# One group of accumulating matmuls moved behind the next step's first transposes in a selective-scan network

## The chip, the cores and the metric

The kernel runs as one program on one core of a Trainium2 chip. The metric is the device time of one execution in microseconds (us), lower is better. A core has five engines that run their own instruction streams and meet at semaphores: TensorE (PE; its weight loads are a row of their own, PEld), VectorE (DVE), ScalarE (ACT), GpSimd (POOL) and SyncE (SP), which issues the DMAs here.

## The reference

Four layers work on an image batch of shape (4, 64, 64, 96). Layers 0 and 1 are two-dimensional selective-scan blocks: a projection in, a 3x3 depthwise convolution, four scans over the 4,096 (or 64 x 33) positions in four directions, a normalization, a gate and a projection out. Layer 1 does this on the image's Fourier transform. Layers 2 and 3 are linear attention and a quantized feed-forward network on the tokens. The scan is what the change touches:

```python
def step(hst, inputs):
    ul, dl, bl, cl = inputs
    dA = jnp.exp(dl[..., None] * A)
    hst = hst * dA + (dl * ul)[..., None] * bl[:, :, None, :]
    y = jnp.einsum('bkdn,bkn->bkd', hst, cl)
    return (hst, y)
```

Every channel d has 16 states n. For each state the recurrence h = h·a + b runs along the positions, with a = exp(delta·A) and b = delta·u·B; the output y is the sum over the 16 states of h·C.

## The kernel before, in words

**Tiling.** Each direction is cut into segments of 512 positions (layer 1: 512, 512, 384, 384 and 320). There are 144 segments. Channels lie on the 128 partitions, in three chunks c. A segment's 16 states are worked in four quarters q of four states j = 0 to 3. A step is one (segment, q, c): four states of one chunk over one segment. There are 144 x 4 x 3 = 1,728 steps, run by one loop (L843), in six phases: two for layer 0 (two images each) and four for layer 1 (one image each).

**What a step needs.** For j = 0 and 1, b is made on ScalarE with positions on the partitions (`make_bx`, L636) and turned round by TensorE: `transposed(st, j)` (L674, matmuls at L678) writes it into a PSUM tile, four matmuls of 128x128 for 512 positions, three for the shorter segments. For j = 2 and 3, b is a product on GpSimd (`front_b`, L695, work at L700). ScalarE makes a with exponentials (L682). VectorE runs the four recurrences one after another (`scan`, L704, work at L710).

**What becomes of h.** The result of j = 0 stays in its PSUM tile. VectorE multiplies it with C (`multiply_kept`, L725, work at L728) into the tile hk, which has two buffers, and ScalarE keeps its last column as the state for the next segment (`keep_state`, L730, work at L735). In every second step of layer 0, and every fourth of layer 1, j = 3 is treated in the same way (`kept`, L519); these are 624 steps. The other states are multiplied on GpSimd (`multiply`, L737, work at L747). TensorE sums all products in a PSUM accumulator `acc`, one per chunk: `add_kept` (L771) for hk, `add_rest` (L766) for GpSimd's products; both call `accumulate` (L749), whose matmuls are at L757 and turn the data back to positions on partitions by passing it against the identity. After the last quarter, `close_chunk` (L783) copies `acc` out (L788) and stores it.

**PSUM tiles.** The b of j = 0 and 1 and the a of j = 2 and 3 share three PSUM tiles in turn (`room`, L671), four uses a step. So the next step's first transposes write into the tile that this step's second scan (j = 1) has read, and its second transposes into the one that the third scan (j = 2) has read. The tile h of GpSimd's products has three buffers: `front_b` for step i+1 writes the buffer of step i-2, which `add_rest` must have read.

**What sets the order.** The order on TensorE, VectorE, ScalarE and GpSimd is written out by hand: the loop from L843 calls each piece where its instruction is to stand, and every engine works through its queue in that order. Only SyncE's order is chosen by the framework. In step i, TensorE's queue holds, from L871: `add_rest` of step i-2; `add_kept` of j = 3 of step i-1, where it has one; `add_kept` of j = 0 of step i (L882); what the first side slot brings (L897); the transposes j = 0 of step i+1 (L899); what the second side slot brings (L902); the transposes j = 1 of step i+1 (L904); what the third side slot brings (L911).

**Side slots.** `slot` (L820) issues work of everything that isn't a scan: preparing the next segment (`prepare`, L553, among it transposes at L612 which ScalarE copies at L615) and a phase's side tasks (projection, convolution, gates, the layers 2 and 3 of another image), at a rate per phase (RATES, L27). A side task yields after each piece; what a piece's matmuls made is read by another engine in a later slot.

Of the kernel before, what the change touches and what calls it, by code (L numbers as in the profile page):

```python
# [523 lines left out]
def scans(tc, ctx, phases, ident):  # L524
# [105 lines left out]
    def fetch_b(z, q):  # L630
        z.b[q] = broadcast(z, 4 * q + 2, 2, 0)

    def fetch_c(z, q):
        z.c[q] = broadcast(z, 4 * q, 4, 1)

    def make_bx(z, q):  # L636

        NI, PI, M, R = z.cfg.NI, z.cfg.PI, z.cfg.M, z.cfg.R
        for j in range(2):
            t = sp.tile([P, NBK, C, P], F32, name=f"bx_{z.nm}_{q}_{j}", tag="bx", bufs=4)  # L640
            z.bx[q, j] = t
            for b, (_, n) in enumerate(z.blocks):
                for i in range(NI):
                    m = i * M + R + 4 * q + j
                    ch = slice(i * PI, (i + 1) * PI)
                    nc.scalar.activation(  # L646
                        t[:n, b, :, ch], z.dut[:n, b, :, ch], AF.Copy, scale=z.bt[:n, b, m : m + 1]
                    )
                    yield
# [15 lines left out]
    def drain(gen):  # L665
        for _ in gen:
            pass
# [3 lines left out]
    def room(st, j):  # L671
        return ps.tile([P, 512], F32, name=f"ab_{st.nm}_{j}", tag=f"ab{next(turn) % 3}")

    def transposed(st, j):  # L674

        pb = st.px[j] = room(st, j)
        for b, (t, n) in enumerate(st.z.blocks):
            nc.tensor.transpose(pb[:, t : t + n], st.z.bx[st.q, j][:n, b, st.c], ident[:n, :n])  # L678
# [7 lines left out]
    def front_x(st):  # L686
        st.ax = sp.tile([P, 2, SM], F32, name=f"ax_{st.nm}", tag="ax", bufs=2)
        for j in range(2):
            exp(st.ax[:, j, : st.z.S], st, 4 * st.q + j)

    def front_y(st, j):
        st.ay[j] = room(st, j)
        exp(st.ay[j][:, : st.z.S], st, 4 * st.q + j)

    def front_b(st):  # L695

        S = st.z.S
        st.h = sp.tile([P, 3, SM], F32, name=f"h_{st.nm}", tag="h", bufs=3)
        for j in range(2):
            nc.gpsimd.tensor_tensor(  # L700
                st.h[:, 1 + j, :S], st.z.du[:, st.c, :S], st.z.b[st.q][:, j, :S], ALU.mult
            )
# [27 lines left out]
    def keep_state(st, j):  # L730
        z = st.z
        n = 4 * st.q + j
        if not z.last:
            e = last(z)
            nc.scalar.copy(z.state[st.c][:, n : n + 1], kept_at(st, j)[:, e : e + 1])  # L735
# [13 lines left out]
    def accumulate(st, hc, first=False, last=False):  # L749
        z = st.z  # L750
        if first:
            z.acc[st.c] = ps.tile([P, 512], F32, name=f"acc_{z.nm}_{st.c}", tag=f"acc{st.c}").rearrange(
                "p (b d) -> p b d", b=NBK
            )
        blocks = list(enumerate(z.blocks))
        for b, (t, m) in blocks[:: -1 if last else 1]:
            nc.tensor.matmul(  # L757
                z.acc[st.c][:m, b, :],
                hc[:, t : t + m],
                ident,  # L760
                start=(first and b == 0),
                stop=(last and b == 0),
                is_transpose=True,
            )

    def add_rest(st):  # L766
        m = 4 - len(st.kept)
        for j in range(m):
            accumulate(st, st.h[:, j], last=(st.q == NQ - 1 and j == m - 1))

    def add_kept(st, j):  # L771
        accumulate(st, st.hk[j], first=(st.q == 0 and j == 0))

    def open_segment(z, before):

        if z.first:
            z.state = [
                sp.tile([P, NST], F32, name=f"state_{z.nm}_{c}", tag=f"state{c}", bufs=2) for c in range(C)
            ]
        else:  # L780
            z.state = before.state
# [17 lines left out]
    with tc.manual_schedule(engines=IN_ORDER):  # L799
        drain(prepare(segs[0]))  # L800
        drain(make_bx(segs[0], 0))
        fetch_b(segs[0], 0)
        fetch_c(segs[0], 0)
        st = steps[0]
        for j in range(2):
            transposed(st, j)
        front_x(st)
        front_b(st)
        before = older = None
        more, pgen, pwants, at, due = Pieces(segs[0], 1, 4), none, None, 0, 0.0  # L810

        def prepare_more(kind):

            nonlocal pwants
            if pwants not in (None, kind):
                return False
            pwants = next(pgen, LATE)
            return True

        def slot(kind, hold=False):  # L820


            nonlocal due
            if hold:
                E.flush()
                return
            prepare_more(kind)
            due = min(due + st.z.ph.rate / 3, 3.0)
            for _ in range(min(int(due), 1 + (due >= 2.0))):
                due -= E.step(kind)  # L830

        def burst():

            if BURST in (pwants, E.wants):
                E.flush()
            if pwants is BURST:
                return prepare_more(BURST)
            if E.wants is BURST:
                E.step(BURST)
                return True  # L840
            return False

        for i, st in enumerate(steps):  # L843
            z, q, c, S = st.z, st.q, st.c, st.z.S
            nxt = steps[i + 1] if i + 1 < len(steps) else None
            if q == 0 and c == 0:
                after = z.after
                fresh = at == 0 or z.ph is not segs[at - 1].ph
                if fresh:
                    z.ph.io["y"] = [z.blk.dram_tile(f"y{j}", (2, z.cfg.L, C * P), z.ph.g) for j in range(2)]  # L850
                open_segment(z, segs[at - 1] if at else None)
                if after:
                    E.require(after.ph.needs[after.k % 2])
                pgen, pwants = prepare(after) if after else none, None
                at += 1
            if fresh and q == 0 and c == C - 1:
                for fn, arg in z.ph.side:
                    E.add((fn, arg), fn(E, arg))
            if c == 0:
                if q + 1 < NQ:  # L860
                    fetch_b(z, q + 1)
                elif after:
                    drain(pgen)
                    more = Pieces(after, 0, 4)
                    fetch_b(after, 0)
            if c == 1:
                if q + 1 < NQ:
                    fetch_c(z, q + 1)
                elif after:
                    fetch_c(after, 0)  # L870
            if older:  # L871
                add_rest(older)
            if before and 3 in before.kept:
                keep_state(before, 3)
                add_kept(before, 3)
            scan(st, 0)
            front_y(st, 2)
            if nxt:
                front_x(nxt)
            multiply_kept(st, 0)  # L880
            keep_state(st, 0)
            add_kept(st, 0)  # L882
            front_y(st, 3)
            long = burst()
            if before:
                multiply(before)
            if nxt:
                front_b(nxt)
            scan(st, 1)
            if nxt:  # L890
                if c == C - 1:
                    drain(more.gen)
                    if q + 2 < NQ:
                        more = Pieces(z, q + 2, 6)
                    elif q + 1 == NQ:
                        more = Pieces(nxt.z, 1, 6)
            slot(None)  # L897
            if nxt:
                transposed(nxt, 0)  # L899
            more.take(skip=long)  # L900
            scan(st, 2)
            slot(None, hold=long)  # L902
            if nxt:
                transposed(nxt, 1)  # L904
            if older and older.q == NQ - 1:
                close_chunk(older)
            scan(st, 3)
            if 3 in st.kept:
                multiply_kept(st, 3)
            more.take(skip=long and c == C - 1)  # L910
            slot(LATE)  # L911
            older, before = before, st
        multiply(before)
        if 3 in before.kept:
            add_kept(before, 3)
        for st in (older, before):
            add_rest(st)
            close_chunk(st)
        E.finish()
# [703 lines left out]
```

## Time and profile before

| What | us |
|---|---|
| median of 3 runs | 11260.47 |
| lowest and highest | 11260.01 and 11280.23 |
| the profiled execution | 11260.07 |
| its span, from first to last instruction | 11258.3 |
| TensorE: matmuls, weight loads busy | 9023.4, 6618.2 |
| VectorE, ScalarE, GpSimd busy | 9756.0, 9354.2, 9614.9 |
| matmuls of L757 from hk (seen as hk_l, k_l, _l) | 4760 + 3628 + 300 |
| matmuls of L757 from h | 16656 |
| matmuls of L678 | 6886 + 5312 + 474 |
| median of one matmul of L757, of L678 | 0.273, 0.273 |

Layer 0's phases begin at about 216 and 2,687 us, layer 1's at 5,130, 6,582, 7,997 and 9,431 us. Ahead of the first step there is only layer 0's first projection and convolution, behind the last (about 10,880 us) the end of the last image.

A row of the profile gives engine, line and operation, the output and inputs by their tile names without numbers, and a duration. The tile hk appears as hk_l, k_l or _l, and the tiles of `room` as ab_l, b_l or _l, since names are cut at the left: they are one kind of tile each. A wait is put down to the instruction whose semaphore came last. Durations of neighbouring matmuls overlap: four in a row at L678 or L757 take 0.60 us together in the median, not four times 0.273.

### The profile page before, as it was taken

How to read it: one execution, taken by the hardware profiler on the slowest of the kernel's cores; microseconds unless marked ns; L12 is line 12 of the kernel's file. 1: busy time of each engine (PE TensorE's matmuls, PEld its weight loads, DVE VectorE, ACT ScalarE, POOL GpSimd, SP SyncE). 2: the span in 40 equal slices, each digit the busy share in tenths (PEclk: the TensorE clock that was granted, in tenths of full speed). 3: DMA queues.
4: the chain of work that ended last, by engine and by line, in shares of the span. 5: the costliest groups of instructions: out<-in, count | busy, mean ns of one | idle time of the engine just before them, and what ended most of it. 6: DMA issues, size and time to landing. Idle time of an engine off the chain costs nothing. (4 is left out here: it accounts for less than half of the span.)

```text
span 11258.3 us, 163664 instructions
## 1 busy us (share of the span) xinstructions
PE 9023.4 (80%) x54944; PEld 6618.2 (59%) x54944; DVE 9756.0 (87%) x10419; ACT 9354.2 (83%) x19456; POOL 9614.9 (85%) x7464
## 2 busy tenths in 40 slices
PE   6678788777888888888888888887788777887775
PEld 2555555555667666656665665655556555655554
DVE  6889999889999998999888787988988889789864
ACT  3779999998898998998778788879888888778853
POOL 2999999888998998999789798988989889889860
PEclk8889999888998998999889899998899888899887
DMA  4655554555665556555554444542244322542242
GB/s 146 146 131 128 133 131 120 153 158 143 163 162 134 137 138 144 133 144 161 154 141 131 128 135 137 172 118 92 96 138 143 102 92 98 157 125 96 82 131 40
DMA packets 1205139, 1466.87 MB, mean 130 GB/s; under 512 B 480839, under 2 KB 1017295, under 8 KB 1145799
## 3 DMA queue, kind: packets, MB, share of 16 engines
q1 hardware_dynamic: 1204295, 1456.40, 47.7%
q8 instruction: 434, 7.11, 0.3%
q14 instruction: 410, 3.36, 0.1%
HBM read 1219.66 MB, written 236.50 MB: 129 GB/s over the span
## 5 line engine op out<-in xcount | busy, mean ns | idle before, releaser
L747 POOL TENSOR_TENSOR h_l<-h_l,bc_l 128x1536 f32<-128x1536 f32 (+2 forms) x1728 | 4784.4, 2769 | 192.1 <-DVE h_l L710 73.1
L700 POOL TENSOR_TENSOR h_l<-du_l,bc_l 128x512 f32<-128x512 f32 (+2 forms) x3456 | 3970.4, 1172 | 620.1 <-PE acc_l L757 581.1
L646 ACT ACTIVATE bx_l<-dut_l,bt_l 128x192 f32<-128x192 f32 (+2 forms) x6272 | 2754.6, 499 | 0.3
L757 PE MATMUL acc_l<-ident,h_l 128*128 128x128 f32 (+1 forms) x16656 | 2430.6, 299 | 243.5 <-POOL h_l L747 242.1
L757 PEld LDWEIGHTS acc_l<-ident,h_l 128*128 128x128 f32 (+1 forms) x16656 | 2130.9, 154 | 836.8 <-POOL h_l L747 384.9
L682 ACT ACTIVATE ax_l<-delta_l,l_alog 128x512 f32<-128x512 f32 (+2 forms) x3456 | 2140.7, 667 | 0.0
L710 DVE TENSOR_TENSOR_SCAN h_l<-b_l,state_l,h_l 128x512 f32<-128x512 f32 (+2 forms) x1388 | 1507.6, 1109 | 123.1 <-ACT b_l L682 104.5
L678 PE MATMUL b_l<-ident,bx_l 128*128 128x128 f32 (+1 forms) x6886 | 1215.4, 295 | 210.2 <-DVE h_l L710 203.2
L678 PEld LDWEIGHTS b_l<-ident,bx_l 128*128 128x128 f32 (+1 forms) x6886 | 854.6, 149 | 816.6 <-DVE h_l L710 464.4
L682 ACT ACTIVATE b_l<-delta_l,l_alog 128x512 f32<-128x512 f32 (+2 forms) x1970 | 1232.6, 626 | 117.2 <-DVE h_l L710 49.4
L710 DVE TENSOR_TENSOR_SCAN b_l<-ax_l,state_l,b_l 128x512 f32<-128x512 f32 (+2 forms) x853 | 967.5, 1134 | 254.8 <-PE b_l L678 253.6
L678 PE MATMUL ab_l<-ident,bx_l 128*128 128x128 f32 x5312 | 896.1, 298 | 223.1 <-DVE h_l L710 213.2
L710 DVE TENSOR_TENSOR_SCAN h_l<-ab_l,state_l,h_l 128x512 f32<-128x512 f32 x803 | 992.7, 1261 | 83.2 <-ACT ab_l L682 48.8
L682 ACT ACTIVATE ab_l<-delta_l,l_alog 128x512 f32<-128x512 f32 x1326 | 912.8, 688 | 152.3 <-DVE h_l L710 81.4
L757 PE MATMUL acc_l<-ident,k_l 128*128 128x128 f32 x4760 | 785.8, 293 | 294.8 <-DVE k_l L728 281.6
L710 DVE TENSOR_TENSOR_SCAN h_l<-ax_l,state_l,b_l 128x512 f32<-128x512 f32 (+2 forms) x853 | 963.2, 1129 | 65.0 <-PE b_l L678 62.7
L678 PEld LDWEIGHTS ab_l<-ident,bx_l 128*128 128x128 f32 x5312 | 654.2, 151 | 583.4 <-DVE h_l L710 414.9
L728 DVE TENSOR_TENSOR k_l<-b_l,bc_l 128x512 f32<-128x512 f32 (+2 forms) x1344 | 832.2, 619 | 47.2 <-DMA bc_l<-l_xd_l 1.0
L297 PE MATMUL pc_l<-pad_l,l_dg 128*128 128x512 f32 (+2 forms) x1656 | 788.1, 564 | 59.5 <-ACT uh_l L275 46.8
L757 PE MATMUL acc_l<-ident,hk_l 128*128 128x128 f32 x3628 | 591.8, 297 | 293.7 <-DVE hk_l L728 280.8
L757 PEld LDWEIGHTS acc_l<-ident,k_l 128*128 128x128 f32 x4760 | 582.8, 150 | 390.7 <-DVE k_l L728 317.9
L710 DVE TENSOR_TENSOR_SCAN ab_l<-ax_l,state_l,ab_l 128x512 f32<-128x512 f32 x496 | 631.9, 1274 | 114.5 <-PE ab_l L678 113.8
(252 smaller groups left out, 14452.2 us busy)
## 6 DMA issues: line engine op xcount, KB each, us to landing
bc_l<-l_xd_l SPq DMA_DIRECT2D x640, 512.0 KB
bc_l<-l_xd_l SPq DMA_DIRECT2D x512, 256.0 KB
bc_l<-l_xd_l SPq DMA_DIRECT2D x128, 1024.0 KB
bc_l<-l_xd_l SPq DMA_DIRECT2D x128, 768.0 KB
us_l<-l_u SPq DMA_DIRECT2D x96, 768.0 KB
l_y<-y_l SPq DMA_DIRECT2D x288, 256.0 KB
yt_l<-l_y SPq DMA_DIRECT2D x264, 192.0 KB
yt_l<-l_y SPq DMA_DIRECT2D x128, 384.0 KB
```

Source lines behind the costliest of these rows:

```text
L297: nc.tensor.matmul(pc[:, : n * 64].rearrange("p (r w) -> p r w", w=64), diag[:, t, :], pad[:, r - p0 + dy : r - p0 + dy + n, dx : dx + 64] ...
L646: nc.scalar.activation(t[:n, b, :, ch], z.dut[:n, b, :, ch], AF.Copy, scale=z.bt[:n, b, m : m + 1])
L678: nc.tensor.transpose(pb[:, t : t + n], st.z.bx[st.q, j][:n, b, st.c], ident[:n, :n])
L682: nc.scalar.activation(out, z.delta[:, st.c, : z.S], AF.Exp, scale=z.blk.A[:, st.c, z.k, n : n + 1])
L700: nc.gpsimd.tensor_tensor(st.h[:, 1 + j, :S], st.z.du[:, st.c, :S], st.z.b[st.q][:, j, :S], ALU.mult)
L710: nc.vector.tensor_tensor_scan(h[:, ::step], a[:, ::step], b[:, ::step], 0.0 if z.first else z.state[st.c][:, n : n + 1], ALU.mult, ALU.add,)
L728: nc.vector.tensor_tensor(hk[:, : z.S], kept_at(st, j), z.c[st.q][:, j, : z.S], ALU.mult)
L747: nc.gpsimd.tensor_tensor(h, h, z.c[st.q][:, 1 : 1 + m, : z.S], ALU.mult)
L757: nc.tensor.matmul(z.acc[st.c][:m, b, :], hc[:, t : t + m], ident, start=(first and b == 0), stop=(last and b == 0), is_transpose=True,)
```

## The change

The call of `add_kept(st, 0)` in the loop moves from L882, ahead of `front_y(st, 3)` and the first side slot, to behind `transposed(nxt, 0)`. `add_kept` issues matmuls on TensorE and nothing else. `multiply_kept` and `keep_state`, which stood ahead of it, stay where they are. In the last step there are no next transposes; there it stands behind the first side slot.

```diff
                 front_x(nxt)
             multiply_kept(st, 0)
             keep_state(st, 0)
-            add_kept(st, 0)
             front_y(st, 3)
             long = burst()
             if before:
...
             slot(None)
             if nxt:
                 transposed(nxt, 0)
+            add_kept(st, 0)
             more.take(skip=long)
             scan(st, 2)
             slot(None, hold=long)
```

TensorE's queue in step i is then: `add_rest` of step i-2; `add_kept` of j = 3 of step i-1; the first side slot; the transposes j = 0 of step i+1; `add_kept` of j = 0 of step i; the second side slot; the transposes j = 1 of step i+1; the third side slot.

## The prediction

> **What bounds the kernel now.** I read the engines' shares first, then the waits of the whole program, then a few microseconds in order of time, and last paired the records of the trace step by step.
>
> The shares, one line per engine: busy microseconds, share of the span, instructions.
>
> ```profile
> PE 9023.4 (80%) x54944; PEld 6618.2 (59%) x54944; DVE 9756.0 (87%) x10419; ACT 9354.2 (83%) x19456; POOL 9614.9 (85%) x7464
> ```
>
> Four engines lie within seven points of each other, none above 87%. No engine's own work is the bound: they run one step of four recurrences in about 6.17 us (mean distance of first scans over the 1,728 steps: 6.40 us in the first two phases, 5.98 us in the other four), and hand it on. What can be won or lost is idle time in the scan stage, which lasts from 290 to about 10,880 us. The chain that ended last breaks off early (no share above 1%), so it doesn't tell.
>
> The waits of the whole program: engine and line, what released it, total us, times, longest.
>
> ```profile
> POOL h_l L700 <- PE acc_l L757: 581.1, 336, 7.7
> ...
> DVE b_l L710 <- PE b_l L678: 313.6, 254, 6.5
> ACT dut_l L615 <- PE pp_l L612: 302.9, 277, 6.5
> PE acc_l L757 <- DVE k_l L728: 281.6, 296, 5.7
> PE acc_l L757 <- DVE hk_l L728: 280.8, 239, 6.7
> ...
> DVE ab_l L710 <- PE ab_l L678: 146.9, 117, 6.7
> ```
>
> The reader is to see a pair. VectorE sits idle for TensorE's transposes of b (313.6 + 146.9, and 20.2 under a cut name, = 480.7 us), almost all before the first scan of a step. And TensorE sits idle for VectorE's product h0·c (281.6 + 280.8 + 30.9 = 593.3 us), with everything else it could do queued behind. The engine that is late in one step was idle in another.
>
> One stalled step in order of time (start, duration, engine, line, operation; in brackets idle time and who ended it):
>
> ```profile
> 3008.99 1.04 PE L757 MATMUL acc_l<-ident,k_l 128*128 128x128 f32 x8
> ...
> 3009.96 1.57 PE L990 MATMUL po<-l_wo,yb_l 64*128 64x96 f32 x12
> ...
> 3011.46 0.66 PE L678 MATMUL b_l<-ident,bx_l 128*128 128x128 f32 x4
> ...
> 3012.16 1.29 DVE L710 TENSOR_TENSOR_SCAN b_l<-ax_l,state_l,b_l 128x512 f32<-128x512 f32 x1 [0.29 <-PE b_l L678]
> ```
>
> The last four of the eight products are this step's first state; then a side task's twelve matmuls; then the transposes for which VectorE has waited 0.29 us.
>
> **What the Trainium skill says.** "Perfetto Trace Analysis", Identifying the Most-Contended Engine: matmul busy time is no measure of TensorE's headroom, the weight loads' share is. The trace agrees: 80% against 59%. "TensorE: Matmul & The Clock Gate", Architectural detail: TensorE's queue lets weight loads pass matmuls in flight, and Part 3 has matmuls start and end in program order. So a product that waits holds up all matmuls behind it; the trace agrees, side work never starts during one of the 593.3 us. The same page, Part 4, gives about 275 ns for a transpose in a kernel's context: the trace has a median of 273 ns, but four in a row are through in 0.60 us, which is what I use. "PSUM — Partial Sum Buffer", Terms: two engines may not even read a bank together. It fits that ScalarE's copy of the state (L735) waits for VectorE's product (159.4 + 147.3 us), though it reads only what the scan wrote.
>
> **The change part by part.**
>
> *Instructions.* None is added or removed: 1,728 groups of four (or three) product matmuls move on TensorE, past the first side slot and the next step's first transposes. The instruction orders of VectorE, ScalarE and GpSimd are the same in both builds. SyncE's 3,809 DMA issues are the same too, 232 of them moved by at most eight places; nothing in the waits puts a DMA issue on the path, so I take zero, with 0.1% either way as the bound.
>
> *The wait removed.* The product's matmuls wait no more: they now stand behind transposes that already wait for the second scan (L710 of j = 1), which VectorE runs after the product. TensorE gets its side slot earlier. In the records the first product waited 600.5 us in 609 steps; the slot between it and the transposes has work in 1,116 of 1,727 steps, 1,233.8 us, 0.71 us a step.
>
> *The gain at the first scan.* I moved the product in each step of the trace and left VectorE's times as they are: transposes start at the later of (TensorE free + slot) and (second scan ends + 0.06 us). They end 0.46 us earlier in the mean, and never later. The first scan waited 482.5 us in 407 steps; limited to each wait, 234.8 us would go. Not all of it stays. First, in stalls that follow each other with TensorE busy throughout, the shift of 0.6 us is won once: 233 episodes, 158.2 us. Second, the *second* transposes aren't earlier, so the second scan may wait instead: at its start 118.7 us of the 234.8 are left, and 85.6 us of the 158.2. I take 118.7 and 85.6 as the two ends for the gain on VectorE, and their middle, 102 us.
>
> *The loss.* With the product between the two transposes, the second ones, the third slot and the sums of the older step (L757 from h) come later where VectorE sets the pace: in 651 of 1,727 steps, by 0.33 us in the mean; earlier by 0.64 us in 119. Against each step's slack that costs GpSimd's products (L700) 37.7 us and gives 19.4 us back, and costs second scans outside stalls 15.9 us: 34 us lost.
>
> *Side work on ScalarE.* L615 waited 160.2 us for transposes from the first slot and 125.9 us from the second. The first come earlier, the second up to 0.6 us later in 139 cases (83 us). I take zero; bounds −80 and +80 us.
>
> *A new wait.* In a step after one with two products (624 steps), VectorE's product now waits for the older product's matmuls to free its buffer. They stand directly behind the transposes that released the scan before it: 0.60 us of matmuls beside a scan of 0.80 to 1.29 us. Zero; if the cover failed, the two scans behind it on VectorE would wait, at most 0.6 us × 624 = 374 us, which the durations exclude.
>
> *Two things left as they are.* In the first quarter of a chunk the product opens the accumulator, which ScalarE must have emptied (L788); coming later, it can only wait less. TensorE's idle time is moved rather than changed, so I leave its granted clock at the 0.898 of this execution.
>
> *The sum.* 102 − 34 = 68 us, against the profiled execution's 11,260.07 us (span 11,258.3 and 1.8 us around it), which is the median of the runs, 11,260.47, to 0.4 us. VectorE, the busiest engine, passes a saving on unless ScalarE or GpSimd is next; an earlier scan also releases TensorE and ScalarE sooner, which the fixed times leave out. I take these as equal: 11,260 − 68 = 11,192, so **11,190 us**, 0.6% less.
>
> **The rivals.**
>
> *A, nothing comes of it.* The 0.6 us gained at the first scan are waited for at the second, or at L700. For it: half of the 234.8 us goes that way already, and GpSimd's 581.1 us of waiting stays. Against it: TensorE's 600 us of idle time do get work. If only the lower end, 85.6, is won and the 34 us doubled by waits that follow: 11,260 − 18 = 11,242 us.
>
> *B, slower.* The delayed second transposes carry the delay through the third slot into the sums at the head of the next step, for which GpSimd waits 336 times. If each of these waits grows by the four matmuls, 336 × 0.60 = 202 us, less 102 gained: +100, 11,360 us. It decides from the point where over half of those waits grow (half: 101 us, even). For it: they are this kernel's largest wait. Against it: of the idle gaps over 0.05 us before L700 that end with the older step's sums (379 in my pairing), TensorE's second transposes end later in 79 and earlier in 26; in the rest TensorE is behind with side work, and the order changes nothing.
>
> *C, more than forecast.* TensorE uses all of its idle time, and the 234.8 us of first-scan waits go with no loss: 11,025 us. Against it: episodes win once.
>
> That the change doesn't do what it says is excluded by the order of the instructions in the changed build.
>
> **How the numbers follow.** Less than 0.2%, 22 us, can't be told from no change. Forecast 0.62, its own range 11,090 to 11,238; A 0.14; B 0.18; C 0.06. Faster: 0.62 + 0.06 = 0.68; same 0.14; slower 0.18. The 80% range goes from 11,090 (68 + 80 from the side work and a little of C) to 11,310, the middle of B's way; outside lie half of C and half of B, 0.12, and some of the forecast's tail.
>
> **What would show it.** Right: the waits of L757 on the product (593.3 us) almost gone, under 100 us; those of the first scan on L678 down from 480.7 to some 300; those of L678 on VectorE's scans up, since the idle time moves there. Second scans waiting for L678 more than now (101.6 us of gaps), and L700 for L757 about 600. Wrong: L700's wait for L757 up by over 100 us (B), or first-scan waits hardly lower (A). If the product on VectorE shows a wait for TensorE, the buffer wait was not covered.

## The result, and the profile after

| Kernel | median us | runs | ratio to the kernel before, 95% interval |
|---|---|---|---|
| before, beside the changed one | 11273.48 | 22 | |
| changed | 11254.05 | 22 | 0.9983 [0.9977, 0.9990] |
| before, on a second occasion | 11267.78 | 37 | |
| changed, on the second occasion | 11251.98 | 13 | 0.9991 [0.9983, 1.0000] |

The change makes the kernel 16 to 19 us faster, 0.1 to 0.2%; on the second occasion the interval reaches 1.0000. The prediction was 11,190 us, 0.6% faster. The absolute time, 11,254 us, lies in the 80% range (11,090 to 11,310), but above the 11,090 to 11,238 that the prediction kept for its own forecast. The direction is right, and the size is a quarter of what was forecast.

The engines' shares in the profile after (busy us, share of the span, instructions):

```profile
PE 8874.6 (79%) x54944; PEld 6606.2 (59%) x54944; DVE 9756.1 (87%) x10419; ACT 9355.0 (83%) x19456; POOL 9616.5 (85%) x7464
```

VectorE, ScalarE and GpSimd work as long as before; VectorE differs by 0.1 us. TensorE's matmul records, whose ends are modelled, add up to 149 us less with the same number of instructions, and its weight loads to 12 us less. What moved is idle time. The waits of the whole program (engine and line, releaser, total us, times, longest):

```profile
POOL h_l L700 <- PE acc_l L757: 562.4, 325, 8.3
PE ab_l L678 <- DVE h_l L710: 495.5, 326, 6.8
PE b_l L678 <- DVE h_l L710: 471.1, 373, 6.2
...
ACT dut_l L615 <- PE pp_l L612: 339.4, 281, 5.9
...
DVE b_l L710 <- PE b_l L678: 211.9, 205, 4.6
...
ACT state_l L735 <- DVE hk_l L728: 137.4, 131, 11.0
DVE ab_l L710 <- PE ab_l L678: 127.9, 89, 6.3
ACT state_l L735 <- DVE k_l L728: 123.1, 167, 3.7
DVE h_l L710 <- PE b_l L678: 120.6, 143, 5.2
...
PE acc_l L757 <- DVE hk_l L728: 12.1, 8, 6.0
```

The forecast mechanism is there. TensorE no longer waits for the product (from 593.3 to 16.5 us with its other names), and VectorE waits less for the first transposes (ab, b and the cut name together: from 480.7 to 355.2 us). But TensorE's idle time has only changed its place: it now waits at the transposes for VectorE's scans (495.5 + 471.1 us). Before, these waits were:

```profile
PE ab_l L678 <- DVE h_l L710: 213.2, 392, 5.4
...
PE b_l L678 <- DVE h_l L710: 203.2, 365, 4.1
```

Paired step by step, TensorE's idle time ahead of the product, the first and the second transposes was 602.0 + 156.9 + 292.5 = 1,051.4 us, and is 2.4 + 932.1 + 116.3 = 1,050.8 us. None of it was used up.

Here is a step of the kernel after in order of time:

```profile
3001.69 1.02 PE L571 MATMUL pp_l<-us_l,l_xpw 128*76 128x512 f32 x2
...
3002.28 1.27 DVE L710 TENSOR_TENSOR_SCAN h_l<-ax_l,state_l,b_l 128x512 f32<-128x512 f32 x1
...
3003.60 0.66 PE L678 MATMUL b_l<-ident,bx_l 128*128 128x128 f32 x4 [0.89 <-DVE h_l L710]
...
3004.10 0.60 PE L757 MATMUL acc_l<-ident,k_l 128*128 128x128 f32 x4
...
3004.53 1.02 PE L571 MATMUL pp_l<-us_l,l_xpw 128*76 128x512 f32 x2
...
3005.39 0.60 PE L678 MATMUL b_l<-ident,bx_l 128*128 128x128 f32 x4
```

The side slot's work (3001.69) runs early, as meant. Then TensorE waits 0.89 us for the second scan all the same. The product (3004.10) and the second slot stand between the two groups of transposes, so the second group comes at 3005.39.

VectorE's idle time, taken from the records by what it precedes, adds up to the difference of the two scan stages (10,651.9 and 10,643.7 us from first scan to last). Small gaps are included, since the product starts 0.034 us behind the scan ahead of it even where nothing holds it up. The first row includes 53 us ahead of the very first scan, the same in both:

| Idle time ahead of | before, us | after, us | difference |
|---|---|---|---|
| first scan | 536.3 | 412.3 | -124.0 |
| second scan | 101.9 | 169.0 | +67.1 |
| product of state 0 | 70.2 | 110.1 | +39.9 |
| third scan | 195.7 | 201.1 | +5.4 |
| fourth scan | 133.8 | 138.7 | +4.9 |
| second product, side tasks | 162.5 | 161.0 | -1.5 |
| sum | | | -8.2 |

These two executions are 8 us apart, less than the medians, but they tell where the gain went: over half comes back at the second scan, and a third at the product. A second execution of the changed kernel repeats the first three rows (412.8, 167.1 and 108.4 us). ScalarE has the same picture. Idle time ahead of the state's copy (L735) fell by 53.7 us; ahead of L615 it grew by 36.3 and ahead of L788 by 18.7 us.

### The profile page after: what moved, and what is told of

Its sections match the earlier page's. It is cut to its first block, busy times and chain, and to the rows that moved or that the text cites. A ratio compares the mean times of both kernels' runs of the same rounds, so it can differ in the third digit from the quotient of the medians.

```text
span 11250.4 us, 163240 instructions
## 1 busy us (share of the span) xinstructions
PE 8874.6 (79%) x54944; PEld 6606.2 (59%) x54944; DVE 9756.1 (87%) x10419; ACT 9355.0 (83%) x19456; POOL 9616.5 (85%) x7464
## 5 line engine op out<-in xcount | busy, mean ns | idle before, releaser
L747 POOL TENSOR_TENSOR h_l<-h_l,bc_l 128x1536 f32<-128x1536 f32 (+2 forms) x1728 | 4782.5, 2768 | 195.2 <-DVE h_l L710 76.6
L700 POOL TENSOR_TENSOR h_l<-du_l,bc_l 128x512 f32<-128x512 f32 (+2 forms) x3456 | 3971.1, 1171 | 598.6 <-PE acc_l L757 562.4
L757 PE MATMUL acc_l<-ident,h_l 128*128 128x128 f32 (+1 forms) x16656 | 2378.3, 295 | 277.0 <-POOL h_l L747 275.6
L757 PEld LDWEIGHTS acc_l<-ident,h_l 128*128 128x128 f32 (+1 forms) x16656 | 2083.4, 152 | 864.5 <-POOL h_l L747 426.7
L678 PE MATMUL b_l<-ident,bx_l 128*128 128x128 f32 (+1 forms) x6886 | 1252.7, 298 | 484.1 <-DVE h_l L710 471.1
L678 PE MATMUL ab_l<-ident,bx_l 128*128 128x128 f32 x5312 | 928.1, 302 | 514.5 <-DVE h_l L710 495.5
L728 DVE TENSOR_TENSOR k_l<-b_l,bc_l 128x512 f32<-128x512 f32 (+2 forms) x1344 | 832.6, 619 | 73.6 <-DMA bc_l<-l_xd_l 3.7
L757 PE MATMUL acc_l<-ident,k_l 128*128 128x128 f32 x4760 | 807.3, 290 | 5.9 <-DVE k_l L728 4.5
L728 DVE TENSOR_TENSOR hk_l<-ab_l,bc_l 128x512 f32<-128x512 f32 x907 | 627.3, 692 | 52.9 <-DMA bc_l<-l_xd_l 5.8
L710 DVE TENSOR_TENSOR_SCAN h_l<-ax_l,state_l,ab_l 128x512 f32<-128x512 f32 x496 | 630.7, 1272 | 29.9 <-PE ab_l L678 29.4
```

What stands on the lines that cost most here:

```text
L700: nc.gpsimd.tensor_tensor(st.h[:, 1 + j, :S], st.z.du[:, st.c, :S], st.z.b[st.q][:, j, :S], ALU.mult)
L710: nc.vector.tensor_tensor_scan(h[:, ::step], a[:, ::step], b[:, ::step], 0.0 if z.first else z.state[st.c][:, n : n + 1], ALU.mult, ALU.add,)
L728: nc.vector.tensor_tensor(hk[:, : z.S], kept_at(st, j), z.c[st.q][:, j, : z.S], ALU.mult)
L747: nc.gpsimd.tensor_tensor(h, h, z.c[st.q][:, 1 : 1 + m, : z.S], ALU.mult)
L757: nc.tensor.matmul(z.acc[st.c][:m, b, :], hc[:, t : t + m], ident, start=(first and b == 0), stop=(last and b == 0), is_transpose=True,)
```

## The experiments

**The new wait: taken away, and made to come in more steps.** Of the 1,728 products on VectorE, 603 have a wait for TensorE after the change. My theory (1 in the expectations) became that it costs a semaphore instruction, not waiting. The instructions of the product's line, before and after, with count and durations in ns:

```profile
L728 DVEq EVENT_SEMAPHORE  x576: 21/21/7846, 216.2 to 10854.9; - x192
```

```profile
L728 DVEq EVENT_SEMAPHORE  x1099: 21/21/3077, 217.4 to 10856.8; - x184
```

There are 523 more, fewer than 603, since some of the further waits share an instruction that holds DMA waits. In steps with the wait the product starts 0.104 us after its scan ends (median), in all others and everywhere before 0.034 us. The older product's matmuls always ended earlier, by 0.03 us at least and 2.95 us in the median. Two scans and products of the kernel after show it:

```profile
3000.30 1.28 DVE L710 TENSOR_TENSOR_SCAN b_l<-ax_l,state_l,b_l 128x512 f32<-128x512 f32 x1
3001.67 0.69 DVE L728 TENSOR_TENSOR k_l<-b_l,bc_l 128x512 f32<-128x512 f32 x1
...
3008.37 1.28 DVE L710 TENSOR_TENSOR_SCAN b_l<-ax_l,state_l,b_l 128x512 f32<-128x512 f32 x1
3009.68 0.69 DVE L728 TENSOR_TENSOR k_l<-b_l,bc_l 128x512 f32<-128x512 f32 x1
```

The first product follows its scan by 3001.67 - 3001.58 = 0.09 us, the second by 0.03. The semaphore instruction of the first lasts 1,847 ns from 2999.8, so it ends 0.05 us behind the scan, and the product starts 0.04 us later. The product must wait for the scan and for TensorE. In all 603 steps the records show the wait for VectorE's own scan in the semaphore instruction, and the wait for TensorE in the product. In the steps that had a semaphore instruction before the change it held only DMA waits, and the gap was 0.034 us too.

Taken away, with a third buffer:

```diff
-        hk = st.hk[j] = sp.tile([P, SM], F32, name=f"hk_{st.nm}_{j}", tag="hk", bufs=2)
+        hk = st.hk[j] = sp.tile([P, SM], F32, name=f"hk_{st.nm}_{j}", tag="hk", bufs=3)
```

> The changed kernel with three buffers for hk instead of two; nothing else differs, and VectorE's product waits for TensorE in no step any more (before: in none, after: in 603 steps). Theory 1 (the new wait costs a semaphore instruction, not waiting): the idle time before the product falls from 71 us to about 11 us, the gap before it from 0.104 to 0.034 us in those steps, 603 x 0.070 = 42 us less on VectorE, and most of that comes through: about 40 us under the changed kernel, 0.994 to 0.996 of the kernel before. Theory 2 (GpSimd and ScalarE set the pace, VectorE's spare time is worth nothing): the time stays within 10 us of the changed kernel, 0.998.

Measured: 11,232.76 us, 0.9977 [0.9971, 0.9984]. Its profile has 576 semaphore instructions at L728 again:

```profile
L728 DVEq EVENT_SEMAPHORE  x576: 21/21/2945, 214.8 to 10821.1; - x192
```

Idle time before the product is back to 67.8 us. The time missed theory 1's 0.994 to 0.996. In more steps, with one buffer for each kept state:

```diff
-        hk = st.hk[j] = sp.tile([P, SM], F32, name=f"hk_{st.nm}_{j}", tag="hk", bufs=2)
+        hk = st.hk[j] = sp.tile([P, SM], F32, name=f"hk_{st.nm}_{j}", tag=f"hk{j}", bufs=1)
```

> The changed kernel with one hk buffer for state 0 and one for state 3, two in all as now; the product then waits for TensorE in 1,619 steps instead of 603, each time for matmuls that have long ended or end beside the scan. Theory 1: 1,016 more semaphore instructions x 0.070 = 71 us more on VectorE, time 40 to 71 us over the changed kernel, 1.002 to 1.005 of the kernel before. Theory 2: as the changed kernel, 0.998.

Measured: 11,266.50 us, 1.0000 [0.9992, 1.0008], with

```profile
L728 DVEq EVENT_SEMAPHORE  x1905: 21/21/4536, 212.9 to 10877.2; - x191
```

and 176.1 us of idle time before the product. The changed kernel and the one with three buffers were then run again on one chip.

> The changed kernel itself, on one chip with the next three. Its time beside that of the kernel with three hk buffers prices the new wait directly: 603 semaphore instructions, about 42 us on VectorE. With the share of 0 to 0.3 that the added VectorE work and the doubled waits have shown, 0 to 13 us apart; with the share of 1 that the prediction took, 42 us. Against the kernel before: 0.998.

> The changed kernel with three hk buffers, again, on one chip with the changed kernel: 0 to 13 us under it if VectorE passes on a small share, 42 us under it if it passes on all. Against the kernel before: 0.9975 to 0.998.

Measured: 11,251.98 and 11,240.00 us, ratios 0.9991 [0.9983, 1.0000] and 0.9976 [0.9967, 0.9985]. So about 40 us of idle time on VectorE are worth 12 us by the medians (about 6 us either way, from the spread of the runs), 17 us by the ratios. In the first set of runs 176.1 - 67.8 = 108 us are worth 34 us by the medians, 0.0023 x 11,264 = 26 us by the ratios. The wait costs VectorE what theory 1 says, but only a quarter to four tenths of that reaches the end, so theory 1's times (1.002 to 1.005 with the wait in nearly each step) were missed too. With the wait in 1,619 of the 1,728 steps the whole gain is gone.

The third buffer by itself, in the kernel before:

> The kernel before with three hk buffers instead of two. Orders and waits on the compute engines are those of the kernel before. If the third buffer helps only by taking away the new wait: the time of the kernel before, ratio 0.999 to 1.001. If it helps by itself (other addresses, other times of freeing): under 0.999.

Measured: 11,275.52 us, 1.0002 [0.9994, 1.0010]. It does nothing without the move.

**What a microsecond on each engine is worth.** The prediction let VectorE pass all of its saving on. Four kernels add a small instruction to each step of the kernel before, on one engine each, and a fifth repeats VectorE's with a larger one. VectorE's:

```diff
+    spare = sp.tile([P, 8, 64], F32, name="spare", tag="spare")
...
             scan(st, 1)
+            nc.vector.memset(spare[:, i % 8], 0.0)
```

> The kernel before with one more VectorE instruction in each of the 1,728 steps, a memset of 128x64 in a spare tile behind the second scan, which waits for nothing and is read by nobody. It measures how much of a microsecond on VectorE reaches the end; the added busy time is read from the profile. Theory 1 as the prediction had it (VectorE passes all on): the time grows by 0.8 to 1.0 of what is added. Theory 4 (four engines share the pace, so that each passes on a part only): by 0.2 to 0.5 of it.

The memset on GpSimd stands just ahead of `scan(st, 1)`, the copy on ScalarE behind `front_y(st, 3)`; on TensorE a transpose is repeated.

```diff
+            nc.gpsimd.memset(spare[:, i % 8], 0.0)
...
+            nc.scalar.copy(spare[:, i % 8, 0:32], ident[:, 0:32])
...
+            if j == 0 and b == 0:
+                nc.tensor.transpose(pb[:, t : t + n], st.z.bx[st.q, j][:n, b, st.c], ident[:n, :n])
```

> The kernel before with one more GpSimd instruction in each step, a memset of 128x64 in a spare tile behind the step's products for the next one, read by nobody. Theory 4: 0.2 to 0.5 of the added time reaches the end. Theory 2 (GpSimd sets the pace): 0.8 to 1.0 of it, and a clearly larger share than VectorE's.

> The kernel before with one more ScalarE instruction in each step, a copy of 128x32 from the identity to a spare tile behind the exponential of state 3. Theory 4: 0.2 to 0.5 of the added time reaches the end. If ScalarE is a cushion, under 0.2.

> The kernel before with the first of each step's four transposes of state 0 run twice (the second overwrites the first with the same values): one more 128x128 matmul in each step, some 0.15 us of TensorE's time by the 0.60 us that four take, 260 us in all. Theory 4: 0.2 to 0.5 of it reaches the end, 50 to 130 us. Theory 1's picture of stalls (407 of 1,728 steps wait for these transposes): 0.24 of it, about 60 us.

> The kernel before with one more VectorE memset of 128x256 in each step, four times the size of the one that added 55 us of busy time; the added time is read from the profile, some 300 to 450 us. If four engines share the pace, 0.1 to 0.4 of it reaches the end; if VectorE has room, under 0.1; if it passes all on once the room is used up, over 0.6.

The shares lines of the kernels with more VectorE work (128x64, then 128x256), more GpSimd, more ScalarE and more TensorE work, one profile each:

```profile
PE 9033.9 (80%) x54944; PEld 6618.3 (59%) x54944; DVE 9810.7 (87%) x12147; ACT 9357.8 (83%) x19456; POOL 9615.7 (85%) x7464
```

```profile
PE 9055.2 (80%) x54944; PEld 6609.3 (58%) x54944; DVE 10063.9 (89%) x12147; ACT 9374.0 (83%) x19456; POOL 9613.7 (85%) x7464
```

```profile
PE 9063.0 (80%) x54944; PEld 6655.2 (59%) x54944; DVE 9762.8 (86%) x10419; ACT 9355.3 (83%) x19456; POOL 9755.7 (86%) x9192
```

```profile
PE 9064.7 (80%) x54944; PEld 6641.9 (59%) x54944; DVE 9763.6 (86%) x10419; ACT 9542.0 (84%) x21184; POOL 9618.0 (85%) x7464
```

```profile
PE 9134.4 (81%) x56672; PEld 6751.1 (60%) x56672; DVE 9755.9 (87%) x10419; ACT 9352.2 (83%) x19456; POOL 9609.6 (85%) x7464
```

Each engine's own entry is compared with the kernel before. For VectorE the busy time says too little: it grew by 54.7 and 307.9 us, but the record of the next instruction, mostly a scan, is shorter there (median 1.256 us at 128x512, then 1.211 and 1.159), and that instruction starts 0.074 and 0.274 us later, which is 128 and 473 us in 1,728 steps. These are in the table. On GpSimd and ScalarE both ways agree. The clock is the mean of the TensorE clock granted in the runs, beside it that of the kernel before. The last column divides the change of time (ratio less one, times the 11,273 or 11,275 us of the runs beside it) by the added time:

| Engine | added us | ratio, 95% interval | clock here and before | share that reaches the end |
|---|---|---|---|---|
| VectorE, small | 128 | 1.0001 [0.9994, 1.0008] | 0.8994, 0.8972 | 0 (-0.05 to 0.07) |
| VectorE, large | 473 | 1.0092 [1.0077, 1.0108] | 0.8985, 0.8978 | 0.22 (0.18 to 0.26) |
| GpSimd | 140.8 | 1.0027 [1.0016, 1.0039] | 0.8970, 0.8972 | 0.22 (0.13 to 0.31) |
| ScalarE | 187.8 | 1.0058 [1.0046, 1.0071] | 0.8942, 0.8972 | 0.35 (0.28 to 0.43) |
| TensorE (weight loads) | 132.9 | 0.9999 [0.9991, 1.0008] | 0.9072, 0.8972 | not told apart from the clock |

Of the three engines that can be read, none passes on more than about a third of its added time, and VectorE, though the busiest, is not ahead of ScalarE. Theory 4 holds for GpSimd, ScalarE and the large VectorE load; the small VectorE load stays below it. The share is measured for added work; for waits saved it may differ.

The time of the kernel with more transposes did not move, but that is no proof that TensorE's time is free. In all its 13 runs the granted clock was 0.906 or higher, in none of the 34 runs beside it above 0.900. Over 330 runs of this study (all kernels with ten or more on an occasion), each set against the mean of its own group, a run with 0.001 more clock is 4.0 us shorter. If the clock is the cause of that, which no run here shows, 0.010 more hides about 40 us (an estimate from these figures), 0.3 of what was added. For the smaller shifts of the clock in the other rows the same estimate gives 9 us (small VectorE load) and 12 us (ScalarE).

**Only half of the move.** The product goes behind the first side slot, but stays ahead of the transposes:

```diff
             slot(None)
+            add_kept(st, 0)
             if nxt:
                 transposed(nxt, 0)
```

(and it is removed from its old place).

> Only half of the move: the product stands behind the first side slot but still ahead of the next step's first transposes. No new wait. From the records of the kernel before, with VectorE's times left: TensorE's idle time before the product gets side work, the first scan's waits fall by only 24 us of 482. Theory 1 (the gain at the first scan comes from the transposes passing the product, not from filling idle time): time 10 to 25 us under the kernel before, ratio 0.998 to 0.999. Theory 3 (filling TensorE's idle time is what helps): as much as the changed kernel or more, ratio 0.998 or less, with the second scan's waits not up.

Measured: 11,273.59 us beside 11,263.88, 1.0010 [1.0003, 1.0016]: slower by a tenth of a per cent. Theory 3 falls. (From here on idle time is counted in gaps of over 0.05 us.) Filling TensorE's idle time with side work helps nothing: its idle time before the product fell from 602.0 to 368.1 us, and the first scan's waits rose from 535.8 to 581.2 us. So the gain needs the transposes to pass the product. That this half is slower at all was foreseen by no theory, and why stays open; its granted clock was lower (mean 0.8958 against 0.8976), which by the estimate above goes with 7 of the 10 us.

**The product behind both transposes,** with three hk buffers (here and in the next kernel the old call is removed):

```diff
             if nxt:
                 transposed(nxt, 1)
+            add_kept(st, 0)
             if older and older.q == NQ - 1:
```

> The product stands behind both transposes of the next step, with three hk buffers so that VectorE has no new wait. From the records of the kernel before: the first scan gains as in the changed kernel, and the second transposes are not delayed, so that 232 of 235 us are left at the second scan instead of 103; but TensorE reaches the older step's sums later, in 818 steps by 0.57 us. Theory 1 with the second transposes as the place where the other half went: second scan's waits back to about 100 us (169 in the changed kernel), time below that of the changed kernel with three hk buffers. Rival (the sums at the head of the next step count for more): L700's wait for L757 up by 100 us or more over 562, time at or above that of the changed kernel with three hk buffers.

Measured: 11,262.61 us, 1.0000 [0.9992, 1.0008], 30 us over the kernel with three buffers that ran beside it. The second scan's waits did fall (163.4 to 124.0 us), but the first scan's rose again (416.0 to 485.3), and GpSimd waited longer for the sums:

```profile
POOL h_l L700 <- PE acc_l L757: 638.8, 343, 8.7
```

That is 83 us more than the 555.8 us with three buffers, and 60 us more than in a second execution of that kernel (579.0). The rival of this experiment was right about the time; its 100 us were more than came. That the sums alone cost the time isn't shown, since the first scan lost as well.

**The second side slot ahead of the product,** with three hk buffers:

```diff
             scan(st, 2)
             slot(None, hold=long)
+            add_kept(st, 0)
             if nxt:
                 transposed(nxt, 1)
```

> The changed kernel with three hk buffers, and the product behind the second side slot instead of ahead of it; it still stands ahead of the second transposes. Theory 5 (on ScalarE, the engine whose added work counted most, what the copy of the state at L735 wins is lost at L615, since the second slot's transposes stand behind the product): waits of L615 back from 336 to about 300 us, L735 as now at 280 to 290, and 0.35 of the 36 us, some 10 us, under the kernel with three hk buffers. Rival (L615's wait is cover for something else): L615 falls and the time stays, within 5 us.

Measured: 11,241.88 us, 0.9978 [0.9970, 0.9986], 2 us from the kernel with three buffers. Idle time before L615 went down from 335.7 to 306.1 us as expected, L735 rose from 281.6 to 299.4 and the second scan's idle time from 172.2 to 223.5 us. So theory 5 was right about L615, but the wait came back in other places and no time was won: the rival holds.

**The sums ahead of the third side slot,** with three hk buffers; `add_rest` goes to the end of the step before (behind the loop, only the last step's sums remain):

```diff
-            if older:
-                add_rest(older)
...
+            if before:
+                add_rest(before)
             slot(LATE)
```

> The changed kernel with three hk buffers, and the sums of the step before (L757 from h) moved from the head of a step to the end of the step ahead of it, in front of the third side slot. GpSimd's product for the next step (L700) waits for these sums, 594 us now, the largest wait. Theory 6 (this wait holds the pace): L700's gaps fall by 200 us or more, time 40 us or more under the kernel with three hk buffers. Rival (four engines share the pace): TensorE then waits for GpSimd's product (L747) instead, and for the same reason the time moves by less than 20 us either way.

Measured: 11,291.26 us, 1.0024 [1.0014, 1.0033], 51 us slower than the kernel with three buffers beside it. GpSimd's waits in this kernel:

```profile
POOL state_l L744 <- DVE h_l L710: 402.8, 289, 10.3
POOL h_l L700 <- PE acc_l L757: 362.8, 227, 7.1
```

In the kernel with three buffers beside it:

```profile
POOL h_l L700 <- PE acc_l L757: 579.0, 335, 8.3
POOL state_l L744 <- DVE h_l L710: 197.7, 122, 10.3
```

The largest wait of all went down by 216 us, and a wait for VectorE's last scan grew by 205. Theory 6 falls. Its rival missed too: it had TensorE waiting longer for GpSimd's product, but these waits (PE, L757 from L747) went from 275.6 to 245.2 us, and it had less than 20 us of change. On VectorE the lost time stands ahead of side tasks, whose matmuls now come behind the sums: 136.4 us of idle time became 199.0. This is the plainest case of what the study shows: a wait on one engine is not time to be had.

## Why the prediction was right or wrong

**The wait removed: right.** The product's waits went from 593.3 to 16.5 us, under the 100 us that the prediction named, and TensorE's waits for the scans rose.

**The gain at the first scan: right in kind, too large. This is the first step that failed.** I took 102 us, as what is left at the second scan, from 85.6 to 118.7 us. The first scan won 124.0 us and the second lost 67.1: 57 us are left. The 234.8 us came from moving the product while VectorE's times stood still; half was realized. The lower sum over episodes, 158.2, was nearer. That about half is lost at the second scan was sized rightly (67 of 124; forecast, 116 of 235). Why the first scan won no more than 124 us stays open: that a shift is won once an episode fits, but no run tests it.

**The new wait: wrong. This is the second step that failed.** The prediction put it at zero: "They stand directly behind the transposes that released the scan before it". TensorE was indeed never late. But the wait itself takes an instruction, which costs up to 0.070 us 603 times. It takes 39.9 us of VectorE's time, the largest single loss that the sum left out, and some 12 us of the kernel's. Its bounds considered only how long one waits, not what waiting costs.

**The loss: wrong place.** L700 was to wait some 18 us longer; it waits 18.7 us less, though two executions with the order of before (581.1, and 597.4 with a third buffer) differ by 16 us themselves. Third and fourth scans lost 10 us. What the second scans lost outside stalls can't be parted from the 67.1 us above.

**Side work on ScalarE: half right.** L615's waits behind the second slot grew by 43 us (125.9 to 169.0), within the bound of 83; those behind the first fell by only 9.

**The passing on: taken too simply, but not a term of its own.** "VectorE, the busiest engine, passes a saving on unless ScalarE or GpSimd is next" was then taken as a share of one. Work added to VectorE passed on 0 to 0.22, and the 40 us that the third buffer saves at the product came out as about 12. What isn't passed on is not lost outside the table, though: VectorE's busy time did not change, so its idle time has to account for the whole difference, and a saving in one row comes back as a longer wait in another. The rows give 57 - 40 - 10 = 7 us for the two executions, of which the stage shows 8, where the forecast had 102 - 34 = 68: 45 us from the gain and 40 us from the new wait, less 24 us because the loss was smaller. The medians show 16 to 19. Even without the new wait, with three buffers, the kernel wins only 28 to 31 us of the 68, so most of what is missing lies in the gain that was reckoned with fixed times.

**The clock: left at 0.898, and it moved.** On the second occasion the changed kernel had 0.8992 in the mean, the kernel before 0.8979. By the estimate above that goes with 5 of the 16 us, a part that the sum put at nothing; it isn't shown that the clock is the cause.

**Readings that the sum does not use.** The scan stage starts at 216 us, not at 290. TensorE's 80% and 59% show that the two figures differ, not which of them measures its headroom. The 275 ns from the Trainium skill ("TensorE: Matmul & The Clock Gate", Part 4) stand there beside a figure for 128x128 bf16, in another kernel; the transposes here are fp32, so that 273 ns is near them confirms nothing.

Of the rivals, A, "nothing comes of it", came nearest: 11,242 us is 18 us less than its 11,260, and the measured difference is 16 to 19, under the 22 us that the prediction counted as no change. That the number fits is luck: half of its mechanism is right, the second scan; L700 isn't, and the new wait, which no rival had, did the rest. B is refuted: L700 didn't grow. C as well: the idle time was moved, not used.

The version with three hk buffers beats both kernels: 0.9977 and 0.9976 of the kernel before in two runs, 12 us under the changed kernel on the same chip.

## What to carry to other kernels

Where several engines are busy to nearly the same degree, measure what a microsecond on each is worth, by adding a small harmless instruction to each step, before pricing a saving at its full size. When an order is changed, list the new waits and count them, even those that will always be met: a wait that pushes another one into an instruction of its own costs time in each step, and a buffer more may remove it. Follow the freed time to the next wait on the same engine before calling it a gain. When a test adds work to TensorE, look at the granted clock of its runs before reading the time.

## What the runs showed that I had not expected

A second wait that was always met made VectorE start 0.104 instead of 0.034 us after the instruction ahead. A semaphore instruction that held only DMA waits cost nothing there. And 1,728 extra transposes in the group that VectorE waits for (132.9 us of weight loads) came with a granted clock of 0.907 instead of 0.897 and left the time where it was, while 187.8 us of small copies on ScalarE, busy for 83% of the span, came with 0.894 and cost 65 us.
